# Four accumulator banks for layer one's plain products, the score bank as a staging place, and an input block prepared ten slots sooner

## The chip, the core and the metric

The kernel runs on one core of a Trainium2 chip. The metric is the device time of one execution in microseconds (us). The core has five engines that run side by side, each taking its own instructions in order: TensorE (PE, the matrix multiplications; PEld is its weight load), VectorE (DVE), ScalarE (ACT), GpSimd (POOL) and SyncE (SP), which here only starts transfers (DMAs). Matrix products go to banks of a small accumulator memory, from which DVE and ACT read them; an engine waits for another through semaphores.

## The reference

A layer norm with ReLU, two layers of a graph network on 128 graphs of 64 nodes with 768 features, and a residual sum. Cut to what matters:

```python
h = relu(layernorm(x))
for l in range(2):
    u_left  = h @ (h @ W_left[l].T).T / sqrt(768)
    u_right = h @ (h @ W_right[l].T).T / sqrt(768)
    u = u_left * triu(adj) + u_right * tril(adj, -1)      # adj has ones on its diagonal
    e = exp(u) * adj
    att = e / (e.sum(-1) + 1e-10)
    h = relu(layernorm2(att @ (h @ W_lin[l].T + b_lin[l])))
out = x + h
```

## The kernel before

**Tiles.** The 128 graphs are cut into 16 blocks of eight graphs (512 rows), and each block into two parts of 256 rows (`TH`). A tile `ht` holds one part, transposed (128 partitions, six chunks of features, 256 rows). Matrices are cut into 256 x 256 blocks; a tile `g` holds one block of a weight matrix, of tokens, or a sum of such blocks.

**Passes.** For each layer, pass one (`pass_one`) computes the products of h with the left and right weights, the scores, and the attention, and pass two applies the attention. Layer index 0 is "layer one" of the title. In pass one the parts form superblocks `SUPER`: the first has two parts (block 0), the others three.

**Plain products.** The first superblock is multiplied directly: `order` lists twelve results (six outputs `w`, two parts `t`), numbered n = 0 to 11. Each is three `product` calls of eight matmuls (L654) that add up in one bank, and is then copied out by ACT (L828) into a tile `m`, the left operand of the scores.

**Chains.** Each later superblock uses a fast matrix multiplication scheme: 40 products `PRODUCTS`, i = 0 to 39, each of a weight sum and a token sum and each of eight matmuls. The weight sums `W_OPS` are made once, during the plain products and just behind them; the token sums `T_OPS`, 38 for each superblock, are made by POOL (L245) in the order of the list, which begins with the sums numbered 9, 10, 11, 12, 13, 14, 15, 16, 17, 18. The first products use the token sums 9, 12, 13, 16, 17, 19. Up to eleven token sums may be held at once, in `g` tiles taken from a list of free ones. Each product is read out of its bank by several operations of DVE (L245, L851) and ACT (L847) that add it into the `m` tiles, as `READS` says. After the fourth product (i = 3) of a superblock the scores of the superblock before are multiplied (L676), and its softmax follows (L684 to L713), whose result goes to memory with eight small transfers ("att").

**Banks.** There are eight. `C`, `D`, `X`, `Y`, `Z`, `V` are one bank each; `scores` (`sc` in the profile) is two. `bank_of(n)` gives the n-th of the six in that order. The plain products of layer one go round `C`, `D`, `X`; those of layer two `X`, `Y`, `Z`. The chain of the second superblock goes round `C`, `D`, `X`, `Y`. While the plain products run, `weights.stage` names three places: for each weight sum on DVE, ACT first copies one operand into the next of these banks (L515), and DVE reads it there (L520 or L245).

**Order.** Every product call takes two slots; `put` registers work at a slot, and `run` emits it when that slot is reached, so that each engine's order is fixed when the program is built. The plain products take slots 0 to 71 (`PLAIN` is 36); `begins(1)` is 72. `turn_of` also decides slot by slot which weight and token sums are emitted, by counters of the time that DVE and POOL are thought to be busy; the batch statistics and transposes of a block count in DVE's.

**Preparing a block.** `prepare(b, slot)` puts into the slots behind `slot`: the statistics of the block's four row tiles on DVE (L336, L337), the deviation on ACT (L395) and its inverse on DVE (L398, L404), four norms on ACT (L410), four transposes on DVE into the single tile `xb` (L463), four stores of `xb` to memory on SP (L459), then eight loads of the next block's rows `x` on SP (L361), and two loads of the transposed parts back into `ht` (L366), from which POOL makes token sums. From block 3 on there is an empty slot behind most of these steps. Blocks 1 and 2 are prepared during the plain products; blocks 3, 4 and 5 at slots 82, 118 and 169, blocks 6, 7 and 8 at 232, 278 and 329, and each following three 160 slots later.

Of the kernel before, what the change touches and what calls it, by code (L numbers as in the profile page):

```python
# [17 lines left out]
def kernel(  # L18
# [24 lines left out]
    NB = B * S // T  # L43
# [23 lines left out]
    def put(slot, *fs):  # L67
        plan.setdefault(slot, []).extend(fs)
# [102 lines left out]
    CHAINS, BANKS = 4, 6  # L171
# [5 lines left out]
    def begins(k):  # L177
        return 0 if k == 0 else 2 * PLAIN + 2 * len(PRODUCTS) * (k - 1)
# [142 lines left out]
    KEEP = {}  # L321
# [299 lines left out]
    def pass_one(l, start, final):  # L621
        with tc.tile_pool(name=f"one{l}", bufs=2, reuse_waits="tile") as sp, \
# [27 lines left out]
            def product(bank, w, t, new, slot):  # L650
                p = bank.rearrange("p (g n) -> p g n", g=2)
                for g in range(2):
                    for c in range(K2):
                        nc.tensor.matmul(p[:, g], w[:, c, g * P:(g + 1) * P], t[:, c, :],  # L654
                                         start=(new and g == c == 0), stop=(c == K2 - 1), skip_group_check=True)
                    if g == 0:
                        turn_of(slot)

            def out_of(bank):
                return bank.rearrange("p (g b s) -> p g b s", g=2, s=S)  # L660

            def into(o):
                v, k, i = o // 6, o // 3 % 2, o % 3
                return M[v][:, i * K2:(i + 1) * K2, :, k, :]
# [56 lines left out]
            if l == 0:  # L721
# [18 lines left out]
                def mid():  # L740
                    for f in turns[1:]:
                        f()
                    load_rows(0, 1, sp)
                    load_rows(0, 2, other)
                    for t in range(2):
                        nc.sync.dma_start(KEPT[0][t], HT[1, 0, t])
                    load_adj(0)
                    cols.extend([column("a_col", ln_a[0]), column("b_col", ln_b[0])])
# [8 lines left out]
            def bank_of(n):  # L757
                n %= BANKS
                return KEEP["CD"][n] if n < 2 else KEEP["XYZV"[n - 2]]

            weights, tokens = Weights(() if l else W_OPS, 2, True), Tokens(l)
# [7 lines left out]
            def turn_of(slot):  # L769
                now = slot * 0.86  # L770
                clock["vector"] = max(clock["vector"], now - 1.0) + sum(getattr(f, "vector", 0.0) for f in plan.get(slot, ()))
                run(slot)
                if fetch and slot >= start["weights"] and slot % 3 and free:
                    i = fetch.pop(0)
                    t = weights.at[FORMS[i]] = free.popleft()
                    nc.sync.dma_start(t, FORM[i])
                if weights.left and slot >= start["weights"]:
                    while clock["vector"] <= now and weights.some(nc.vector):
                        clock["vector"] += 0.62
                    if clock["pool"] <= now and start["pool"] <= slot < start["tokens"]:  # L780
                        if weights.some(nc.gpsimd, 40):
                            clock["pool"] = max(clock["pool"], now) + 1.35
                if clock["pool"] <= now + 1.5 and tokens.step(slot):
                    clock["pool"] = max(clock["pool"], now) + 1.35
# [4 lines left out]
            def prepare(b, slot, step=1):  # L789
                if (l, b) not in XR:  # L790
                    load_rows(l, b, sp)
                end = put_all(slot + 1, [f for f in transpose_rows(l, b, sp) if step > 1 or f is not None], 1)
                if b + 1 < NB and (l, b + 1) not in XR:
                    put(end + (8 if b == 2 else 0), lambda: load_rows(l, b + 1, sp))
                for t in range(2):
                    p = 2 * b + t
                    k = where[p][0]
                    before = p - 6
                    at = end + 3 + t
                    lag = 22 if b > 2 else 16  # L800
                    if before >= 0:
                        at = max(at, begins(where[before][0] + 1) + 2 * SCORED + 3)
                    put(at, lambda p=p: load_part(1, l, p))
                    put_all(at + lag + 6 * t, affine_part(1, l, p))
                    follow.setdefault(k, []).append(at + lag + (7 + 6 * t if l else 0))
                    if len(follow[k]) == len(SUPER[k]):
                        tokens.ready[k] = max(follow[k])
# [2 lines left out]
                follow[1] = [14, 14]  # L810
                put_all(4, affine(1, l, 1))
            for b, at in [(b, start[b]) for b in ((2,) if l else (1, 2))] + [
                    (b, begins(1) + (0 if b > 3 else 10, 46, 97)[b % 3] + 160 * (b // 3 - 1)) for b in range(3, NB)]:
                put(at, lambda b=b, at=at: prepare(b, at, 1 if b < 3 else 2))

            order = [(0, 0), (1, 0), (0, 1), (1, 1)] + [(w, t) for w in range(2, 6) for t in range(2)]
            slot = 0
            for n, (w, t) in enumerate(order):
                bank = KEEP["XYZ"[n % 3]] if l else bank_of(n % 3)
                for j in range(3):  # L820
                    tok = HT[1, l, t][:, j * K2:(j + 1) * K2, :]
                    product(bank, weights.at[3 * w + j], tok, j == 0, slot)
                    weights.used(3 * w + j)
                    if j == 2:
                        if n == 0 and mid:
                            mid()
                            weights.stage = [KEEP[b] for b in "YZV"]
                        nc.scalar.copy(into(6 * t + w), out_of(bank))  # L828
                    turn_of(slot + 1)
                    slot += 2  # L830
# [405 lines left out]
    def final_of(l):  # L1236
# [14 lines left out]
        return final  # L1251

    pass_one(0, {"weights": 0, "pool": 8, "tokens": 60, 1: 16, 2: 30}, final_of(0))
    pass_two(0, {11: lambda: later(load_raw(1), 1)})
    pass_one(1, {"weights": 3, "tokens": 50, 2: 10}, final_of(1))
    pass_two(1, {})

# [28 lines left out]
```

## Time and profile before

| what | value |
|---|---|
| median of 3 runs | 2698.18 us (2697.36 to 2700.32) |
| the profiled execution | 2704.83 us |
| span of its instructions | 2701.9 us |
| mean granted TensorE clock | 0.988 |

The profile is one execution. A row of a view in order of time is: start and duration in us, engine, line and operation, the tiles (result <- operands, buffer numbers left out), shapes, how many instructions were merged, and in brackets how long the engine had been idle before and what ended that. "issue" stands where no releaser is seen. Ends of matmuls are modelled, so rows overlap a little. A row of the view by stretches is: the stretch, its length, then the busy time and count of PE, PEld, DVE, ACT and POOL, the granted TensorE clock (1.00 is full), the share of the DMA engines' time in use, and GB/s.

### The profile page before, as it was taken

To read this page: it belongs to the slowest core of one execution; us is meant where nothing else is said; L and a number is where in the kernel's file an instruction comes from. 1 tells how busy PE (TensorE), PEld (TensorE's weight loads), DVE (VectorE), ACT (ScalarE), POOL (GpSimd) and SP (SyncE) were. 2 spreads that over 40 slices of the span, in tenths; PEclk is the share of its full clock that TensorE was granted. 3 is DMA by queue.
4 is the path that set the end of the run, shared out by engine and by line. 5 is a ranking of instruction groups with operands and counts; after the bars stand their busy time and mean duration, and the time that the engine had idled before them with its cause. 6 is when DMAs were issued, how large, how long until landed. Compare 5 with 4: busy or idle time off the path is not lost. (4 is left out here: it accounts for less than half of the span.)

```text
span 2701.9 us, 46786 instructions
## 1 busy us (share of the span) xinstructions
PE 2615.5 (97%) x18042; PEld 2229.1 (83%) x18042; DVE 1765.2 (65%) x2800; ACT 925.8 (34%) x1941; POOL 1725.6 (64%) x1326
## 2 busy tenths in 40 slices
PE   9889999999999899999899999999999979999998
PEld 8778888888887788888678888888888868888886
DVE  7868868776778445554424766776766685666667
ACT  5512222222213144445452212222222315455543
POOL 4756757666667547766215666676666666787786
PEclk9999999999999999999999999999999999999999
DMA  7353443334321344446786443353442105655655
GB/s 215 81 138 80 115 102 92 86 91 123 80 68 62 120 129 155 144 152 205 210 232 181 104 111 86 85 121 91 115 114 68 64 12 156 183 158 159 180 160 149
DMA packets 263358, 336.52 MB, mean 125 GB/s; under 512 B 56290, under 2 KB 195298, under 8 KB 263138
## 3 DMA queue, kind: packets, MB, share of 16 engines
q1 hardware_dynamic: 246338, 325.28, 44.0%
q10 hardware_dynamic: 16800, 8.26, 1.1%
q8 instruction: 144, 2.36, 0.4%
q14 instruction: 76, 0.62, 0.1%
HBM read 218.11 MB, written 115.34 MB: 123 GB/s over the span
## 5 line engine op out<-in xcount | busy, mean ns | idle before, releaser
L245 POOL TENSOR_TENSOR g<-ht 128x512 f32<-128x512 f32 x584 | 769.1, 1327 | 523.6 <-ACT ht L377 135.4
L245 POOL TENSOR_TENSOR g<-g,g 128x512 f32<-128x512 f32 x295 | 378.8, 1292 | 139.9 <-DVE g L245 42.6
L245 POOL TENSOR_TENSOR g<-ht,g 128x512 f32<-128x512 f32 x256 | 339.9, 1335 | 154.7 <-PE X L654 40.3
L934 PE MATMUL Z<-g,g 128*128 128x256 f32 x1024 | 248.5, 385 | 18.3 <-ACT hl L300 9.8
L654 PE MATMUL C<-g,g 128*128 128x256 f32 x1008 | 243.3, 385 | 15.3 <-DVE m L245 7.7
L654 PE MATMUL X<-g,g 128*128 128x256 f32 x1008 | 241.0, 382 | 9.3 <-ACT m L828 4.1
L934 PEld LDWEIGHTS Z<-g,g 128*128 128x128 f32 x1024 | 194.4, 193 | 50.8 <-issue 12.0
L654 PEld LDWEIGHTS C<-g,g 128*128 128x128 f32 x1008 | 191.8, 192 | 46.7 <-POOL g L245 9.4
L654 PEld LDWEIGHTS X<-g,g 128*128 128x128 f32 x1008 | 191.4, 191 | 38.4 <-issue 4.9
L654 PE MATMUL Y<-g,g 128*128 128x256 f32 x912 | 216.5, 380 | 0.0
L654 PE MATMUL D<-g,g 128*128 128x256 f32 x880 | 208.4, 380 | 4.8 <-issue 2.8
L654 PE MATMUL Z<-g,g 128*128 128x256 f32 x864 | 204.7, 380 | 0.0
L377 ACT ACTIVATE ht<-ht,b_col,a_col 128x256 f32<-128x256 f32 x384 | 195.2, 591 | 24.1 <-DMA ht<-h 20.3
L245 DVE TENSOR_TENSOR m<-m,D 128x512 f32<-128x512 f32 x180 | 118.5, 679 | 116.1 <-ACT m L847 98.3
L654 PEld LDWEIGHTS Y<-g,g 128*128 128x128 f32 x912 | 174.2, 191 | 24.0
L654 PEld LDWEIGHTS D<-g,g 128*128 128x128 f32 x880 | 167.0, 190 | 29.1 <-issue 3.7
L934 PE MATMUL X<-g,g 128*128 128x256 f32 x768 | 185.6, 384 | 0.0
L654 PEld LDWEIGHTS Z<-g,g 128*128 128x128 f32 x864 | 163.5, 190 | 23.3 <-issue 0.5
L654 PE MATMUL V<-g,g 128*128 128x256 f32 x768 | 181.4, 379 | 0.0
L934 PEld LDWEIGHTS X<-g,g 128*128 128x128 f32 x768 | 148.3, 193 | 21.5 <-issue 0.6
L245 DVE TENSOR_TENSOR hl<-hl,Y 128x512 f32<-128x512 f32 (+1 forms) x136 | 89.0, 654 | 115.4 <-PE Y L934 96.6
L1134 POOL TENSOR_TENSOR z<-z,b 128x768 f32<-128x768 f32 x62 | 112.6, 1828 | 78.5 <-DVE z L1131 77.2
(215 smaller groups left out, 4728.9 us busy)
## 6 DMA issues: line engine op xcount, KB each, us to landing
ht<-h SPq DMA_DIRECT2D x126, 768.0 KB, 6.4
h<-xb SPq DMA_DIRECT2D x124, 384.0 KB, 5.9
z<-z SPq DMA_DIRECT2D x128, 192.0 KB, 3.1
x<-z SPq DMA_DIRECT2D x128, 192.0 KB, 5.4
xr<-in_x_dram SPq DMA_DIRECT2D x120, 192.0 KB, 3.8
out_dram<-xr SPq DMA_DIRECT2D x120, 192.0 KB, 2.7
x<-in_x_dram SPq DMA_DIRECT2D x112, 192.0 KB, 5.6
g<-form SPq DMA_DIRECT2D x40, 256.0 KB, 5.1
```

Of the source, the lines that this page charges most:

```text
L245: (eng.tensor_add if sign == "+" else eng.tensor_sub)(o, a, b)
L377: nc.scalar.activation(ht, ht, AF.Relu, bias=cols[1][:, c:c + 1], scale=cols[0][:, c:c + 1])
L654: nc.tensor.matmul(p[:, g], w[:, c, g * P:(g + 1) * P], t[:, c, :], start=(new and g == c == 0), stop=(c == K2 - 1), skip_group_check=True)
L934: nc.tensor.matmul(p[:, n], b[t][:, c, r * P:(r + 1) * P], w[s][:, c, :], start=(i in FIRST and i not in PRELOAD and n == c == 0), stop=(c ...
L1134: nc.gpsimd.tensor_add(zs[k], zs[k], rows["b"])
```

## The change

```diff
             for b, at in [(b, start[b]) for b in ((2,) if l else (1, 2))] + [
-                    (b, begins(1) + (0 if b > 3 else 10, 46, 97)[b % 3] + 160 * (b // 3 - 1)) for b in range(3, NB)]:
+                    (b, begins(1) + (0 if b > 3 or l == 0 else 10, 46, 97)[b % 3] + 160 * (b // 3 - 1)) for b in range(3, NB)]:
                 put(at, lambda b=b, at=at: prepare(b, at, 1 if b < 3 else 2))
...
             for n, (w, t) in enumerate(order):
-                bank = KEEP["XYZ"[n % 3]] if l else bank_of(n % 3)
+                bank = KEEP["XYZ"[n % 3]] if l else bank_of(n % CHAINS)
...
-                            weights.stage = [KEEP[b] for b in "YZV"]
+                            weights.stage = [KEEP["Z"], KEEP["V"], KEEP["scores"][:, 0]]
                         nc.scalar.copy(into(6 * t + w), out_of(bank))
```

`CHAINS` is 4. In layer one the plain products now go round `C`, `D`, `X`, `Y`; the staged copies go round `Z`, `V` and the first of the two score banks; and block 3 is prepared at slot 72 instead of 82. Layer two keeps its banks and its slots.

In the order of the instructions, POOL has the same sequence as before (some sums lie in other `g` tiles). On DVE the four statistics of block 3 stand between the last weight sums and the first reads of the chain, and its four transposes ahead of the softmax's normalization instead of behind it. On ACT its deviation and norms stand earlier by some evictions. On SP the four stores of block 3 and the eight loads of block 4's rows stand ahead of the eight att stores of the first superblock instead of behind them. PE has the same products in the same order.

## The prediction

> **What bounds the kernel now.** I read the page first, then the instructions in order of time on TensorE (PE), ScalarE (ACT), GpSimd (POOL), VectorE (DVE) and the SP queue for the first 210 us, and last the busy time by stretches. Only layer one's first 180 us are touched, so the averages say little by themselves:
>
> ```profile
> span 2701.9 us, 46786 instructions
> ...
> PE 2615.5 (97%) x18042; PEld 2229.1 (83%) x18042; DVE 1765.2 (65%) x2800; ACT 925.8 (34%) x1941; POOL 1725.6 (64%) x1326
> ```
>
> PE is busy 97% of the span, so what can be won is its idle time and its slow clock. Here is PE around the change:
>
> ```profile
> 53.65 5.34 PE L654 MATMUL X<-ht,g 128*128 128x256 f32 x24
> 62.14 6.82 PE L654 MATMUL C<-ht,g 128*128 128x256 f32 x24 [3.15 <-ACT m L828]
> ...
> 79.16 1.89 PE L654 MATMUL C<-g,g 128*128 128x256 f32 x8
> 83.89 1.97 PE L654 MATMUL D<-g,g 128*128 128x256 f32 x8 [2.85 <-issue]
> 89.91 3.75 PE L654 MATMUL X<-g,g 128*128 128x256 f32 x8 [4.06 <-ACT m L828]
> 93.46 2.99 PE L654 MATMUL Y<-g,g 128*128 128x256 f32 x8
> 96.38 4.13 PE L676 MATMUL sc<-m,ht 128*32 128x95 f32 x192
> 101.54 1.97 PE L654 MATMUL C<-g,g 128*128 128x256 f32 x8 [1.03 <-ACT m L847]
> ...
> 127.51 1.89 PE L654 MATMUL Y<-g,g 128*128 128x256 f32 x8
> ...
> 149.88 3.78 PE L654 MATMUL C<-g,g 128*128 128x256 f32 x8 [5.72 <-DVE m L245]
> ...
> 161.77 1.89 PE L654 MATMUL D<-g,g 128*128 128x256 f32 x8
> ...
> 180.86 4.60 PE L676 MATMUL sc<-m,ht 128*32 128x95 f32 x211
> ```
>
> The plain products n = 0 to 11 are the rows of 24 matmuls (5.2 us each when they follow one another); the last begins near 74 and product 0 of the first chain (i = 0) at 79.16. There are two trouble spots. The first is 59 to 101: PE waits for evictions (L828) at n = 9, i = 1 and i = 2. The second is one stall of 5.72 at i = 28. From i = 4 (101.54) to i = 19 (127.51) fifteen products take 25.97, so 1.73 is the undisturbed pitch.
>
> **The change part by part.** Every engine issues the same instructions as before. New are the bank names of twelve products, of their evictions and of the staged sums; the place of block 3's work in the DVE and ACT orders; and on SP the four stores of block 3 and eight x loads of block 4, which now go ahead of the eight att stores.
>
> *Four banks.* An eviction is one ACT copy in a queue full of staging copies:
>
> ```profile
> 61.51 0.58 ACT L828 COPY m<-C 128x512 f32<-128x512 f32 x1
> ...
> 72.34 0.58 ACT L828 COPY m<-X 128x512 f32<-128x512 f32 x1
> ...
> 83.21 0.58 ACT L828 COPY m<-D 128x512 f32<-128x512 f32 x1
> ...
> 89.19 0.58 ACT L828 COPY m<-X 128x512 f32<-128x512 f32 x1
> ...
> 100.31 1.09 ACT L847 ACTIVATE m<-C 128x512 f32<-128x512 f32 x2 [10.05 <-PE sc L676]
> ...
> 115.00 0.30 ACT L395 ACTIVATE sd<-mv,eps_in 128x4 f32<-128x4 f32 x1 [5.68 <-DVE mv L337]
> ```
>
> These are the evictions of n = 6, 8, 10 and 11, then the first of the chain, and block 3's deviation. ACT takes them late because of its own queue, never because PE is late, so their times stay. With four banks a product waits for the eviction four back: n = 10 for n = 6 (62.1), i = 0 for n = 8 (72.9). So n = 9 follows at 59.0, the wait of 3.15 and its slow clock (6.66 to the next row instead of 5.18) go, and the plain products end at 74.5, 4.7 sooner. i = 1, 2, 3 now need n = 9, 10, 11, the last evicted at 89.8. Staging in the score bank costs nothing: ACT copies into it and DVE reads it as before with Y, and its last read is over before the DVE row at 92.57 below, ahead of the scores.
>
> Here the gain meets the next wait. i = 0, 1, 2, 3 use token sums 9, 12, 13, 16, the first, fourth, fifth and eighth that POOL makes:
>
> ```profile
> 76.98 2.53 POOL L245 TENSOR_TENSOR g<-ht 128x512 f32<-128x512 f32 x2
> ...
> 84.33 2.51 POOL L245 TENSOR_TENSOR g<-ht 128x512 f32<-128x512 f32 x2 [1.93 <-DVE g L520]
> 89.37 2.62 POOL L245 TENSOR_TENSOR g<-ht,g 128x512 f32<-128x512 f32 x2 [2.54 <-DVE g L520]
> ...
> 94.29 1.65 POOL L245 TENSOR_TENSOR g<-ht 128x512 f32<-128x512 f32 x1 [0.63 <-DVE g L520]
> ```
>
> The first pair holds sums one and two, the second five and six, the third seven and eight; they wait for tiles that the weight sums on DVE give back, a stream that the change leaves alone. So i = 0 waits until 78.2, i = 2 until 85.6, and i = 3 until 92.0 (89.37 + 2.62), later than its eviction. Today i = 3 starts at 93.46, so only 1.5 us is left of 4.7. The clock takes part of that:
>
> ```profile
> 82.00:86.00 4.00, 1.97 (x8) 1.44 (x8) 3.79 (x8) 3.97 (x8) 2.07 (x3) 1.00 1.01 207
> 86.00:90.00 4.00, 0.09 (x1) 0.12 (x1) 3.90 (x8) 3.76 (x8) 1.46 (x2) 0.86 0.55 122
> 90.00:94.00 4.00, 4.00 (x10) 3.19 (x11) 3.97 (x4) 0.26 (x1) 3.58 (x3) 0.50 0.00 0
> 94.00:98.00 4.00, 4.00 (x88) 3.28 (x90) 0.81 (x2) 0.00 (x0) 3.63 (x3) 0.79 0.01 2
> ```
>
> After the 4.06 us gap the granted clock (the column behind POOL's) was 0.50, and i = 2 and i = 3 took 3.55 and 2.92 to the next row, 3.0 over two pitches. The 3.15 gap cost 1.5, the 5.72 gap 1.9 (3.78 instead of 1.89). The new gap before i = 3 is 92.0 less the end of i = 2 (about 87.4), 4.6 us, so it costs 1.5 to 3.0; I take 2.5, between its neighbours. i = 3 and the scores then end at 92.0 + 1.73 + 3.93 (96.38 to 100.31) + 2.5 = 100.2, against 100.31: a gain of 0.1, from -0.4 to +1.1, and +2.6 if the clock stays up.
>
> [...]
>
> *Block 3 ten slots sooner.* This is DVE and SP around the second stall:
>
> ```profile
> 92.57 1.64 DVE L520 SCALAR_TENSOR_TENSOR g<-g,g 128x512 f32<-128x512 f32 x1
> ...
> 102.41 0.69 DVE L245 TENSOR_TENSOR m<-m,D 128x512 f32<-128x512 f32 x1 [7.59 <-ACT m L847]
> ...
> 120.27 0.42 DVE L700 TENSOR_REDUCE s<-adj 128x4 f32<-128x256 f32 x1
> ...
> 131.29 0.95 DVE L463 STREAM_TRANSPOSE xb<-x 128x768 f32<-128x768 f32 x1
> ...
> 137.29 0.69 DVE L245 TENSOR_TENSOR m<-m,Y 128x512 f32<-128x512 f32 x1 [0.44 <-PE Y L654]
> 148.01 1.02 DVE L336 BATCH_NORM_STATS2 st<-x 128x6 f32<-128x384 f32 x2 [10.03 <-DMA x<-in_x_dram]
> 149.07 0.21 DVE L337 BATCH_NORM_AGGREGATE mv<-st 128x2 f32<-128x12 f32 x1
> ...
> 180.88 0.68 DVE L245 TENSOR_TENSOR m<-m,Y 128x512 f32<-128x512 f32 x1
> ```
>
> ```profile
> 77.09 7.16 SPq L361 DMA_DIRECT2D x<-in_x_dram x8
> 127.17 5.20 SPq L713 DMA_DIRECT2D att<-wm x8
> 132.47 5.15 SPq L459 DMA_DIRECT2D h<-xb x4
> 137.72 6.84 SPq L361 DMA_DIRECT2D x<-in_x_dram x8
> ```
>
> The chain today: the fourth transpose of block 3 ends at 132.2, its stores go out, then the x loads of block 4 at 137.72; their first half is there at 148.01, 10.3 later. DVE takes instructions in order and stood 10.03 at block 4's statistics with the bank reads of i = 24 and later behind it; PE ran on through its free banks for 4.3 and then stood 5.72 at i = 28.
>
> Afterwards three of block 3's four statistics (1.23 each) stand in DVE's idle time before 102.41. The fourth transpose stands directly behind the row at 120.27, so it ends at 120.7 + 0.95 = 121.6 or a little sooner: what now precedes it lost four statistics (4.9; three into the idle time, the fourth by about 104) and gained three transposes (2.9). I take 121. The stores then run to 126.3 and block 4's x is there at 126.3 + 10.3 = 136.6. DVE arrives at about 137.0 (137.98 less the gains ahead of it). The wait goes, by a small margin, and there are 4.3 us of bank cover behind that.
>
> What PE gets: from 127.51 (i = 19) to 161.77 (i = 33) fourteen products took 34.26 against 14 x 1.73 = 24.2. The loss of 10.0 holds the 5.72, the slow clock behind it, and about 0.9 at i = 20 to 22, where the transposes held up the bank reads; these are out of the way too. What is late next is DVE at the end of the chain. From 148.01 to its last read at 181.56 it works 33.5 almost without a pause; from 137.0 that reaches 170.5, and the scores, today at 180.86, would begin at 170.8. I charge 0.5 (0 if it holds, 2.6 if x comes 3 us later).
>
> The added waits: ACT's deviation and norms of block 3 now stand ahead of the eviction of i = 7, whose bank is needed again at i = 11, four pitches or 6.9 later; today ACT stands idle for 5.68 ahead of that deviation. POOL's tenth sum (94.29) waits for the DVE sum of 92.57, now behind one statistic: 1.2 later, used at i = 5, four us on. I cost both at nothing; without that cover they would cost about 1 each.
>
> **Sum.** 0.1 + 10.0 - 0.5 = 9.6 sooner. The profiled execution took 2704.83 (its span 2701.9 and 2.9 around it), which gives 2695.2; it stood 6.65 above the median of the runs, 2698.18, for which I forecast 2688.6, by itself 2686 to 2692.
>
> **The rivals.**
> - *The bank gain is kept.* If the tokens come with the faster PE, or the clock stays up, the first part brings 2.6 to 4.7: 2685. Against it: POOL's waits are all on DVE.
> - *x comes only partly sooner.* The x loads share the DMA engines with the stores; if they land at 143, DVE waits 6, PE 1.7 and a slow clock of 1.5, and the end of the chain slips: about 5 gained, 2693. Today's 10.3 already holds the same stores in front.
> - *Nothing arrives.* DVE is the true bound from 102 to 181, and what PE no longer waits at i = 28 it waits at the scores: 2698. For it: the margin of 0.3 above; against it: DVE has 10 us of plain idle in between.
> - *Slower: block 3's x is late.* DVE would stand at block 3's statistics at 92.6 with the last weight sums and all bank reads behind it, and POOL and PE behind these. It costs what x comes after 102.4, and outweighs what the change brings from 112 on, over 20 us late: with x at 118, 16 lost against 10 won, 2704. Against it: the loads went out from 77.09 to 84.25, and the DMA share fell from 0.55 to 0.00 after 90.
>
> **How the numbers follow.** Forecast 0.57, bank gain kept 0.10, partly 0.14, nothing 0.11, slower 0.08. The measurement can tell 0.2%, 5.4 us, from no change. Faster: 0.57 + 0.10 + half of partly = 0.74; same 0.07 + 0.11 = 0.18; slower 0.08. From 2684 to 2696 lie the first two cases and most of the third, about 0.79.
>
> **What would show it.** Right: no wait for ACT L828 at n = 9; i = 3 at 92 with POOL as the releaser and a granted clock near 0.5; the x loads on SP before att, near 126; no wait of DVE for x near 137; an unbroken row of products to the scores near 171. Wrong: a DVE wait on x of more than 4 us, a wait of PE before those scores of more than 3, or scores of the first superblock ending before 98 or after 102.

## The result, and the profile after

| | before | changed |
|---|---|---|
| median of 11 runs each | 2698.31 us | 2691.68 us |
| lowest to highest | 2694.95 to 2706.13 | 2687.73 to 2696.23 |
| ratio, with its 95% interval | | 0.9972 [0.9964, 0.9980] |
| the profiled execution (span) | 2704.83 (2701.9) | 2692.07 (2690.1) |

The changed kernel is 6.6 us faster, by the interval 5.4 to 9.7; 9.6 was forecast. Its median lies 3.1 us above the forecast of 2688.6 and 0.3 under the end of the range, 2692. Measured again (5 runs, against 9 of before) the ratio was 0.9965 [0.9951, 0.9978], medians 2692.39 and 2699.91.

PE in order of time, in the changed kernel (start, duration, instruction, and in brackets the idle time and its end):

```profile
60.26 5.34 PE L654 MATMUL D<-ht,g 128*128 128x256 f32 x24
...
70.62 5.34 PE L654 MATMUL Y<-ht,g 128*128 128x256 f32 x24
76.99 1.99 PE L654 MATMUL C<-g,g 128*128 128x256 f32 x8 [1.03 <-POOL g L245]
81.17 1.99 PE L654 MATMUL D<-g,g 128*128 128x256 f32 x8 [2.19 <-POOL g L245]
84.32 1.99 PE L654 MATMUL X<-g,g 128*128 128x256 f32 x8 [1.15 <-POOL g L245]
90.70 3.54 PE L654 MATMUL Y<-g,g 128*128 128x256 f32 x8 [4.39 <-POOL g L245]
94.17 4.13 PE L676 MATMUL sc<-m,ht 128*32 128x95 f32 x192
99.33 1.97 PE L654 MATMUL C<-g,g 128*128 128x256 f32 x8 [1.03 <-ACT m L847]
...
125.30 1.89 PE L654 MATMUL Y<-g,g 128*128 128x256 f32 x8
...
149.48 1.89 PE L654 MATMUL D<-g,g 128*128 128x256 f32 x8
...
168.56 4.60 PE L676 MATMUL sc<-m,ht 128*32 128x95 f32 x211
```

The plain products run without a wait (n = 9 at 60.26, n = 11 at 70.62). Every wait of PE for ACT's evictions between 59 and 92 has become a wait for POOL. Behind the first scores the row is unbroken: from i = 19 (125.30) to i = 33 (149.48) fourteen products take 24.18, where they took 34.26.

POOL, DVE and SP in order of time, in the changed kernel, one fence each:

```profile
83.00 2.50 POOL L245 TENSOR_TENSOR g<-ht 128x512 f32<-128x512 f32 x2 [1.88 <-DVE g L520]
88.04 2.61 POOL L245 TENSOR_TENSOR g<-ht,g 128x512 f32<-128x512 f32 x2 [2.53 <-DVE g L520]
```

```profile
95.78 0.21 DVE L337 BATCH_NORM_AGGREGATE mv<-st 128x2 f32<-128x12 f32 x1
100.20 0.69 DVE L245 TENSOR_TENSOR m<-m,D 128x512 f32<-128x512 f32 x1 [4.21 <-ACT m L847]
...
117.14 0.97 DVE L463 STREAM_TRANSPOSE xb<-x 128x768 f32<-128x768 f32 x1
...
134.14 0.69 DVE L245 TENSOR_TENSOR m<-m,Y 128x512 f32<-128x512 f32 x1 [0.44 <-PE Y L654]
134.74 1.01 DVE L336 BATCH_NORM_STATS2 st<-x 128x6 f32<-128x384 f32 x2
```

```profile
118.13 5.17 SPq L459 DMA_DIRECT2D h<-xb x4
123.47 9.42 SPq L361 DMA_DIRECT2D x<-in_x_dram x8
133.00 5.53 SPq L713 DMA_DIRECT2D att<-wm x8
```

The eighth token sum ends at 88.04 + 2.61 = 90.65, and i = 3 starts at 90.70, at a granted clock of 0.53 from 92 to 94 us. Three of block 3's statistics fill DVE's idle time before 100.20, the fourth transpose ends at 118.1, and the x loads of block 4 are issued from 123.47; DVE finds x there at 134.74, where it had stood for 10.03.

Everything here lies some 1.3 us earlier on the clock of the execution than in the first trace, as POOL's last group of weight sums shows. These are its rows before and in the changed kernel:

```profile
70.70 6.34 POOL L245 TENSOR_TENSOR g<-g,g 128x512 f32<-128x512 f32 x5 [5.99 <-ACT Y L515]
```

```profile
69.38 6.33 POOL L245 TENSOR_TENSOR g<-g,g 128x512 f32<-128x512 f32 x5 [5.97 <-ACT Z L515]
```

I therefore count from the start of that group. The edits leave its place in the orders alone and change only the bank of the staged copy that releases it; it begins at 69.48 to 70.70 in the four traces with three banks and at 68.96 to 71.00 in the six with four. The table has, for each trace, that start (G), the start of the first and of the second superblock's scores, and the end of the span:

| trace | G | G to first scores | first to second scores | second scores to end |
|---|---|---|---|---|
| before | 70.70 | 25.68 | 84.48 | 2521.0 |
| before, second trace | 69.48 | 25.62 | 84.97 | 2517.5 |
| banks alone | 69.94 | 24.79 | 83.65 | 2513.8 |
| block 3 alone | 70.68 | 25.37 | 74.40 | 2517.6 |
| block 3 alone, second trace | 70.34 | 25.21 | 74.39 | 2517.2 |
| changed | 69.38 | 24.79 | 74.39 | 2521.5 |
| changed, second trace | 69.84 | 25.05 | 75.41 | 2520.2 |
| x behind att | 71.00 | 24.76 | 78.32 | 2517.5 |
| scores early | 68.96 | 20.51 | 76.66 | 2524.9 |
| without token sums | 70.37 | 22.84 | 75.32 | 2514.1 |

The first two differences show what the edits do. Behind the second scores all these kernels issue the same work, and still it took 2513.8 to 2524.9; two traces of one kernel differ there by up to 3.5 us. I take the last column for scatter between executions.

### The profile page after: what moved, and what is told of

It reads as the page before. It is cut to its first block, busy times and chain, and to the rows that moved or that the text cites. A ratio compares the mean times of both kernels' runs of the same rounds, so it can differ in the third digit from the quotient of the medians.

```text
span 2690.1 us, 46793 instructions
## 1 busy us (share of the span) xinstructions
PE 2609.2 (97%) x18042; PEld 2225.5 (83%) x18042; DVE 1763.0 (66%) x2800; ACT 925.7 (34%) x1941; POOL 1725.7 (64%) x1326
## 5 line engine op out<-in xcount | busy, mean ns | idle before, releaser
L676 PE MATMUL sc<-m,ht 128*32 128x95 f32 x6144 | 141.7, 250 | 21.4 <-issue 18.3
```

The costliest lines, as they stand in the source:

```text
L676: nc.tensor.matmul(p[h * S + e:h * S + e + 32, q, e:e + 95], ht[:, c, b * S + e:b * S + e + 32], mb[:, e:e + 95], start=(c == 0), stop=(c ...
```

## The experiments

**The parts.** The four banks and the new staging place, with block 3 back at its old slot. This edit and the next are shown against the changed kernel:

```diff
-                    (b, begins(1) + (0 if b > 3 or l == 0 else 10, 46, 97)[b % 3] + 160 * (b // 3 - 1)) for b in range(3, NB)]:
+                    (b, begins(1) + (0 if b > 3 else 10, 46, 97)[b % 3] + 160 * (b // 3 - 1)) for b in range(3, NB)]:
```

> The four banks and the score bank as a staging place, with block 3 prepared at its old slot. Theory A (the token sums of POOL take over at i = 3, so the banks bring little): about 1 us faster than before; the plain products run without a wait, i = 3 starts when the eighth token sum of POOL ends, two or more us behind its bank's eviction, at a granted clock near 0.5; the scores of the first superblock start 1 to 2 us sooner; the 5 to 6 us wait of PE at i = 28 stays. Theory B (the banks are the main gain, and the stall at i = 28 in the profiled execution of before was a matter of that one execution): 5 us or more faster, and no or little wait at i = 28.

Measured: 2699.45 against 2700.12, ratio 1.000 [0.9991, 1.0009]. PE in this kernel:

```profile
91.27 3.53 PE L654 MATMUL Y<-g,g 128*128 128x256 f32 x8 [4.38 <-POOL g L245]
94.73 4.22 PE L676 MATMUL sc<-m,ht 128*32 128x95 f32 x192
...
148.01 3.78 PE L654 MATMUL C<-g,g 128*128 128x256 f32 x8 [5.41 <-DVE m L245]
```

The wait for POOL is the same as in the changed kernel, 0.8 to 0.9 us are won up to the first scores (24.79 against 25.68 and 25.62), and the stall at i = 28 stays. Theory B falls.

Block 3 sooner, with the banks and staging places of before:

```diff
-                bank = KEEP["XYZ"[n % 3]] if l else bank_of(n % CHAINS)
+                bank = KEEP["XYZ"[n % 3]] if l else bank_of(n % 3)
...
-                            weights.stage = [KEEP["Z"], KEEP["V"], KEEP["scores"][:, 0]]
+                            weights.stage = [KEEP[b] for b in "YZV"]
```

> Block 3 prepared ten slots sooner, three banks and the old staging places as before. Theory A (the gain is block 4's x, which comes sooner): 6 to 10 us faster than before; PE still waits about 3 us at n = 9 and for the evictions at i = 1 and 2; DVE does not wait for x before block 4's statistics and PE does not wait at i = 28; from i = 19 to i = 33 it takes 24.2 us instead of 34.3. Theory B: 1 to 2 us faster.

Measured: 2689.91 against 2700.12, ratio 0.9962 [0.9949, 0.9974], 7.0 to 13.8 us faster. PE and DVE in this kernel:

```profile
62.12 5.45 PE L654 MATMUL C<-ht,g 128*128 128x256 f32 x24 [2.30 <-ACT m L828]
...
89.88 3.75 PE L654 MATMUL X<-g,g 128*128 128x256 f32 x8 [3.18 <-ACT m L828]
```

```profile
136.62 1.01 DVE L336 BATCH_NORM_STATS2 st<-x 128x6 f32<-128x384 f32 x2
```

The eviction waits are all there, and yet the first scores come 25.37 and 25.21 after G, against 24.79 and 25.05 with four banks. (In the second trace of this kernel PE comes to n = 9 late and does not wait there.) The wait for x is gone, and with it the 10 us between the scores (74.40 against 84.48). The gain of the change is this edit.

**Whether the stall belongs to before.** The kernel before, unchanged:

> The kernel before, once more. Theory A: DVE waits for block 4's x again and PE stands at i = 28; the wait may differ by some us between executions, since it hangs on transfers, and this execution lies nearer the median than the first profile did. Theory B: little or no wait at i = 28.

Measured: 2700.7 in a single run. Its x and its stall:

```profile
147.39 1.02 DVE L336 BATCH_NORM_STATS2 st<-x 128x6 f32<-128x384 f32 x2 [10.70 <-DMA x<-in_x_dram]
```

```profile
149.26 3.51 PE L654 MATMUL C<-g,g 128*128 128x256 f32 x8 [6.39 <-DVE m L245]
```

With the kernel that has the banks alone, that makes three traces with the old slot, with PE standing 5.72, 6.39 and 5.41 us. It is no accident of one execution.

**How much lateness the free banks cover.** The changed kernel, with the loads of block 4's x three slots later, behind att and ahead of the ht loads:

```diff
-                    put(end + (8 if b == 2 else 0), lambda: load_rows(l, b + 1, sp))
+                    put(end + (8 if b == 2 else 3 if (l, b) == (0, 3) else 0), lambda: load_rows(l, b + 1, sp))
```

> The changed kernel, but SP issues the loads of block 4's x behind the eight att stores, as before, and ahead of the ht loads. Theory A (the transposes set the time of x, and the bank cover takes a late x of up to 4 us): the x loads are issued about 129 instead of 123.5, DVE waits 1 to 5 us for x at about 135, PE waits less than 1 us at i = 28, the time is that of the changed kernel within 1 us. Rival (the place on SP's queue is what counts): DVE waits 8 us or more and PE 4 or more, and most of the gain is lost.

Measured: 2694.54 in a single run. SP, DVE and PE:

```profile
124.99 9.55 SPq L713 DMA_DIRECT2D att<-wm x8
134.64 4.73 SPq L361 DMA_DIRECT2D x<-in_x_dram x8
```

```profile
141.57 1.02 DVE L336 BATCH_NORM_STATS2 st<-x 128x6 f32<-128x384 f32 x2 [5.16 <-DMA x<-in_x_dram]
```

```profile
143.44 1.99 PE L654 MATMUL C<-g,g 128*128 128x256 f32 x8 [0.85 <-DVE m L245]
146.52 1.99 PE L654 MATMUL D<-ht,g 128*128 128x256 f32 x8 [1.09 <-DVE m L245]
...
151.16 1.99 PE L654 MATMUL Y<-ht,g 128*128 128x256 f32 x8 [0.92 <-DVE m L245]
```

Neither theory met it. The att stores took 9.55 to issue, so x went out at 134.64, not 129. It was there at 141.57, 6.9 behind its first issue, where the kernel before took 10.3; the time of issue alone does not say when x is there. PE's wait at i = 28 is under 1 us, as theory A had it, but two more follow, and the second scores come 3.9 us late (78.32 against 74.39). Of DVE's wait of 5.16 us, then, only 1.2 was covered. The clock had no part in this: the eight matmuls behind each of the three waits took 1.99, what they took behind the wait of 1.03 in the changed kernel, at a granted clock of 1.00 (76 to 80 us).

Free banks postpone the loss; DVE, which has little idle time behind that point, hands it on at the next products. From x to the second scores DVE was busy 31.4 of 32.4 us here (141.57 to 174.00) and 31.1 of 33.8 in the changed kernel (134.74 to 168.50), so 1.6 us of its own idle time was used up, about what was covered. In the kernel before as little was covered of the 10.03: 34.26 less 24.18 is a loss of 10.08, with 0.95 of it ahead of the stall, so 9.1 was paid. There the slow clock behind the stall (3.78 instead of 1.89, at a granted clock of 0.50 from 148 to 152 us) lies in that sum, and the share of each is not separated.

In these traces the place of x on SP's queue is thus worth 3.9 of the 10.1 us between the two scores. The other 6.2 (84.48 less 78.32) came with x behind att, from the sooner place of block 3's work.

**What holds the first four products.** The changed kernel, with products 0 to 11 of the second superblock reading a token block instead of their token sum. It leaves the sums out of these products, so it does not compute the reference:

```diff
                     w, tok = weights.need(f), tokens.need(k, t)
+                    if (l, k) == (0, 1) and i < 12 and t >= 9:
+                        tok = tokens.value(k, 0)
```

> The changed kernel, in which products 0 to 11 of the second superblock of layer one multiply a token block in place of their token sum (POOL still makes the sums). Theory A: PE waits for POOL nowhere up to i = 3; i = 0 follows the plain products at once, i = 3 starts at its bank's eviction, about 2.3 us sooner against POOL's last weight sums, and so do the scores. Rival (ACT's evictions hold i = 3 anyway): i = 3 starts where it does in the changed kernel.

Measured: 2684.36 in a single run. PE:

```profile
78.51 1.99 PE L654 MATMUL D<-ht,g 128*128 128x256 f32 x8 [0.72 <-ACT m L828]
83.61 1.97 PE L654 MATMUL X<-ht,g 128*128 128x256 f32 x8 [3.11 <-ACT m L828]
89.50 3.78 PE L654 MATMUL Y<-ht,g 128*128 128x256 f32 x8 [3.92 <-ACT m L828]
93.21 5.11 PE L676 MATMUL sc<-m,ht 128*32 128x95 f32 x192
```

No wait for POOL is left, and the evictions are the releasers again. i = 3 starts 19.13 after G (89.50 - 70.37), in the changed kernel 21.32 (90.70 - 69.38): 2.2 sooner, as theory A had it. The two limits thus lie 2.2 us apart, which is why four banks alone could win so little. Of these 2.2 only 1.0 is left at the second scores (98.16 against 99.18 from G), since the first scores took 5.11 instead of the 4.13 that they took in the changed kernel, there at a granted clock of 1.00 (94 to 98 us). The rest of the 8 us by which this run was faster is not explained; behind the second scores it had one of the shortest remainders.

The changed kernel, with the scores ahead of that fourth product:

```diff
-                    if i == SCORED:
+                    early = 2 if (l, k) == (0, 1) else SCORED
+                    if i == early:
                         scores(k - 1)
-                    if i >= SCORED:
+                    if i >= early:
```

> The changed kernel, but the scores of layer one's first superblock stand behind three products of the chain instead of four, so they no longer wait for the product of the eighth token sum. Theory A (the token sums of POOL, one after another, set the pace there): the scores start at the eviction of n = 11, 5 to 6 us sooner; then PE waits for POOL's token sums near i = 6 and 7, and of the 5 to 6 us some 2 are left from i = 12 on; about 2 us faster than the changed kernel. Rival (the evictions set the pace): all of the 5 us stay.

Measured: 2691.02 against 2699.91, ratio 0.9965 [0.9952, 0.9977]; the changed kernel, which ran beside it, had 0.9965 too. PE:

```profile
83.78 3.78 PE L654 MATMUL D<-g,g 128*128 128x256 f32 x8 [5.21 <-POOL g L245]
...
89.47 4.13 PE L676 MATMUL sc<-m,ht 128*32 128x95 f32 x192
...
99.46 1.99 PE L654 MATMUL X<-g,g 128*128 128x256 f32 x8 [0.49 <-POOL g L245]
102.04 1.99 PE L654 MATMUL Y<-g,g 128*128 128x256 f32 x8 [0.59 <-POOL g L245]
```

The scores start 4.3 us sooner against G (20.51 against 24.79; in this execution the tokens' load was late, POOL waited 3.35 for it, and i = 1 waited 5.21). Then PE waits for POOL at i = 6 and 7, and up to the second scores 2.0 us are left (97.17 against 99.18). So POOL's token sums, one after another, are what the beginning of the chain goes by. The 2 us do not show in the medians; it is not shown to be faster than the changed kernel.

**Do the banks cost something later?** The changed kernel and block 3 alone, once more and side by side:

> The changed kernel once more. Measured from POOL's last group of weight sums (the one that ends a wait of 6 us for ACT), the scores of the first superblock start 24.8 us later, as in the first profile, and those of the second 74.4 after that. The time against before lies 6 to 11 us lower.

> Block 3 sooner alone, once more, on the same chip as the changed kernel. Theory A (the banks bring 0.9 us at the first scores and nothing later): the changed kernel is 0 to 2 us faster than this one, which the measurement can hardly tell. Rival (the banks cost something later): this one is 2 us or more faster than the changed kernel.

Measured: 0.9965 [0.9951, 0.9978] for the changed kernel, 0.9968 [0.9955, 0.9980] for block 3 alone, medians 2692.39 and 2692.30. No cost and no gain of the banks can be told. In the trace of the changed kernel the scores came 25.05 after G, and those of the second superblock 75.41 later, not 74.4; the first scores show where the 1 us went:

```profile
91.17 3.78 PE L654 MATMUL Y<-g,g 128*128 128x256 f32 x8 [4.38 <-POOL g L245]
94.89 5.15 PE L676 MATMUL sc<-m,ht 128*32 128x95 f32 x192
```

5.15 instead of 4.13, and 3.78 instead of 3.54 for i = 3, behind the same gap (4.38 and 4.39): the slow spell was longer here. In the first trace the granted clock was 0.53 from 92 to 94 us and 1.00 from 94 to 96.

## Why the prediction was right

- *The banks free the plain products, and the token sums take over.* The takeover came as forecast. From POOL's group to the end of the eighth sum the forecast had 21.29 (91.99 - 70.70); i = 3 started 21.32 behind it. But the plain products ended only 2.0 us sooner from G (6.4 behind it instead of 8.5), not 4.7. The wait at n = 9 that the forecast took away was that execution's: with three banks it was 3.15, 1.58, 2.30 and none in four traces. That this did not matter is the token sums' doing.
- *The clock takes part of that.* I took 2.5 us, between 1.5 and 3.0. In the first trace it was 1.7 (3.47 from i = 3 to the scores, against 1.73), in the second 3.0 (3.72, and 1.0 more up to i = 4). Both lie in the range. The part up to i = 4 brought 0.9, -0.4 and, with the banks alone, 0.8 us (30.84 from G to i = 4 before; 29.95, 31.23 and 30.04), where 0.1, from -0.4 to 1.1, was forecast.
- *Block 4's x comes in time.* The fourth transpose ended 48.7 after G (forecast 50.3), the loads were out 5.4 behind it, and DVE did not wait, though SP needed 9.42 for the eight loads instead of 6.84. It did not wait in five traces. In the run with the scores early, where i = 23 started 2.0 us sooner from G (60.81 against 62.83), it waited 0.6. By that the margin of the changed kernel was about 1.4 us (an estimate: 2.0 less 0.6, if x was there at the same time from G in both). It held, with little to spare.
- *The 10.0 us from i = 19 to i = 33.* 10.1 came.
- *0.5 for DVE at the end of the chain.* Not needed: from i = 33 to the scores 19.08, before 19.09.
- *4.3 us of bank cover.* This step was wrong, and the result did not depend on it: the late x showed 1.2 of 5.16 covered. The rival of a partly late x used that cover too (1.7 of waiting and 1.5 of slow clock for a DVE wait of 6), yet its total came out near: it had about 5 of 9.6 gained, so some 4.6 lost, and 3.9 was lost for 5.16. What it charged at the end of the chain, where DVE hands its delay on, made up for the cover.
- *The sum.* Up to the second scores the first traces differ by 11.0 counted from G (110.16 and 99.18), the second trace of the changed kernel by 9.7; forecast were 9.6. The median of the first eleven runs shows 6.6, that of the second five 7.5, whose intervals hold 9.6 (9.7 is the end of the first). So the mechanism and the sum hold in the traces, and the medians show less of it. Why they do is not settled; the remainder behind the second scores varies by more than that from trace to trace, and both traces of the changed kernel have a long one.

## What to carry to other kernels

When more buffers remove a wait, look up when the second operand of the same instruction is ready: here the token sum stood 2.2 us behind the free bank, so the banks were worth less than 1 us. When an engine that takes its work in order waits for a load and has little idle time behind it, the engine that it feeds pays most of the wait: here 3.9 of 5.16 us, with four banks between the two. And finishing sooner what a load has to wait for was worth the whole change; the load's place ahead of eight smaller stores on the same queue was 3.9 us of it.

## What the runs showed of the hardware that was not expected

PE was slow also behind gaps that are not the longest, and not each time. For comparison: in the first traces eight matmuls took 1.89 to 1.99 where the granted clock was 1.00 (before from 140 to 144 us, changed from 76 to 80) and 3.78 where it was 0.50 (before from 149.88). With three banks the gap before i = 1 was 3.00 us in each of three traces; the eight matmuls behind it took 1.96 in one (before, second trace) and 2.84 and 3.17 in the others (block 3 alone):

```profile
82.67 1.96 PE L654 MATMUL D<-g,g 128*128 128x256 f32 x8 [3.00 <-issue]
```

```profile
83.87 2.84 PE L654 MATMUL D<-g,g 128*128 128x256 f32 x8 [3.00 <-issue]
```

```profile
83.53 3.17 PE L654 MATMUL D<-g,g 128*128 128x256 f32 x8 [3.00 <-issue]
```

With four banks a gap of 2.32 before i = 0 was followed by slow matmuls (banks alone), and one of 2.40 was not (changed, second trace):

```profile
77.55 3.47 PE L654 MATMUL C<-g,g 128*128 128x256 f32 x8 [2.32 <-POOL g L245]
```

```profile
77.43 1.99 PE L654 MATMUL C<-g,g 128*128 128x256 f32 x8 [2.40 <-POOL g L245]
```

So gaps that are equal within 0.1 us differ in what follows them, here and in the slow spells of 1.7 and 3.0 us behind the same gap of 4.4. Nor does the length of a gap tell by itself: the matmuls were slow behind 2.32 us and behind two gaps of 3.00, and not behind 2.40, a third gap of 3.00, and 3.11 (i = 2 without token sums, 1.97). Why is open.

Each superblock's scores can hold a wait that nothing in the profile explains. This is the second superblock's in the changed kernel:

```profile
175.85 3.38 PE L676 MATMUL sc<-m,ht 128*32 128x95 f32 x77 [2.69 <-issue]
```

Over the whole span these waits add up to 15.6 to 20.2 us in the ten traces, so they can be a part of the scatter behind the second scores (11.1 us between the traces), but not all of it. What causes them was not tried.
